# Adding the softmax row sums of four partition quadrants on VectorE instead of with a TensorE matmul, in a fused attention and convolution kernel

## Chip, cores, metric

One core of a Trainium2 chip. The metric is the device time of one execution in microseconds (us). TensorE is PE in the profile (PEld is its weight load, which runs beside the matmuls), VectorE is DVE, ScalarE is ACT, GpSimd is POOL. PSUM is the memory in which this kernel's matmuls put their results; it is handed out in buffers, here called slots. The granted clock is the share of TensorE's full speed that the profile shows as granted. Medians are of several executions.

## The reference

Sixteen images of 128 channels and 32x32 pixels pass two layers. Layer 0 is attention with four heads, each as wide as the image's 128 channels; layer 1 is two 3x3 convolutions on 4-bit inputs and weights, each followed by a batch norm over all images. Cut to what matters:

```python
def _L0_conv_ref(x, w_qkv, b_qkv, w_out, b_out):
    qkv = jnp.einsum('bchw,oc->bohw', x, w_qkv) + b_qkv[None, :, None, None]
    qkv = qkv.reshape(b, nh, 3 * c, h, w)
    q, k, v = (qkv[:, :, :c], qkv[:, :, c:2 * c], qkv[:, :, 2 * c:])
    # ... q, v to (b*nh, 1024, c), k to (b*nh, c, 1024)
    scores = jnp.einsum('bnc,bcm->bnm', q, k) * c ** (-0.5)
    attn = jax.nn.softmax(scores, axis=-1)
    out = jnp.einsum('bnm,bmc->bnc', attn, v)
    # ... heads side by side
    out = jnp.einsum('bchw,oc->bohw', out, w_out) + b_out[None, :, None, None]
    return out + x

def _L1_conv_ref(x, w1, w2, gamma1, beta1, gamma2, beta2):
    out = conv3x3(act_quant(x), weight_quant(w1))
    out = batchnorm(out, gamma1, beta1)
    out = conv3x3(act_quant(out), weight_quant(w2))
    out = batchnorm(out, gamma2, beta2)
    return out + x
```

## The kernel before

There are 64 heads (16 images of 4), and each goes through eight steps of 128 keys. In a step TensorE makes the scores `pss` (keys on partitions), ScalarE takes their exponential `e`, and TensorE gathers `psa`, the values weighted by `e`. The row sums of the softmax are not taken by TensorE: VectorE adds the eight `e` tiles into `es` (128 x 1024) and reduces `es` in transposed 32x32 blocks to `part` (128 x 32). Each 32-partition quadrant of `part` then holds a sum over its own quarter of the keys, so the four quadrants are still to be added. Before, that is the matmul `psr` with a constant `quad` of ones and zeros, which also repeats the result in every quadrant. The reciprocal, a broadcasting transpose to `rb`, and the multiply and accumulate into `acc` follow.

```python
P, Q, N, NCH, NH, B = 128, 32, 1024, 8, 4, 16
vp   = pool("vo", NCH + 3)             # 11 buffers: an image has 8 vo tiles
smp  = pool("small", 4)
ps_s = pool("ps_s", 2, space=PSUM)     # pss
ps_a = pool("ps_a", 1, space=PSUM)     # psa: one buffer for each half
ps_m = pool("ps_m", 2, space=PSUM)     # psu, psv, psr, psc share two slots
sums = once.tile([P, B * NH, N // Q], F32, name="sums")

def project_v(b, j):                   # for the next image, two tiles per head
    ps = ps_m.tile([P, NH * P], F32, tag="mm", name=f"psv_{b}_{j}")
    nc.tensor.matmul(ps, lhsT=xt[b][:, ts(j, P)], rhs=bt_sb.rearrange(...), ...)
    vos[b, j] = vp.tile([P, NH * P], F32, tag="vo", name=f"vo_{b}_{j}")
    nc.vector.tensor_copy(vos[b, j], ps)                       # L333

def attend(g, j):
    # ... psa matmuls with vos[b, j] and e; es added on VectorE
    if j == NCH - 1:
        nc.vector.tensor_copy(av[:, ts(0, HALF)], psa[g][0])   # L372
        nc.scalar.copy(av[:, ts(1, HALF)], psa[g][1])
        part = smp.tile([P, N // Q], F32, tag="part", ...)
        nc.vector.tensor_reduce(part, es..., AX.X, ALU.add, apply_transpose=True)
        es[g, "part"] = part

def normalise(g):                      # three steps after the head's last scores
    b, h = heads[g]
    ps = ps_m.tile([P, N // Q], F32, tag="mm", name=f"psr_{g}")
    nc.tensor.matmul(ps, lhsT=quad, rhs=es.pop((g, "part")), start=True, stop=True)
    rinv = sums[:, g, :]
    nc.vector.reciprocal(rinv, ps)
    rb = rbp.tile([P, N], F32, tag="rb", name=f"rb_{g}")
    nc.vector.transpose(rb, rinv.unsqueeze(2).to_broadcast([P, N // Q, Q]))
    # ... acc += av * rb; after head 3 the image is complete: x += acc + bias

# ... first convolution of finished images between the steps, the last ones at
#     the end; then a check that no sum over- or underflowed:
nc.vector.tensor_reduce(ext[:, 0:1], flat, AX.X, ALU.min)      # flat = all of sums
nc.vector.tensor_reduce(ext[:, 1:2], flat, AX.X, ALU.max)
```

The eight `vo` tiles of an image are all in use until the last head's steps come by. With 11 buffers only three tiles of the next image can be copied out early. The fourth and fifth (`psv_3`, `psv_4`) stay in the two `ps_m` slots until `attend` of the current image's fourth head frees the first `vo`. Until then no further `psv` can start.

## Time and profile before

| | before |
|---|---|
| median of 3 runs | 2197.61 us (2197.31 to 2199.77) |
| profiled span | 2195.9 us |
| mean granted TensorE clock | 0.989 |
| busy PE / DVE / ACT | 97% / 53% / 32% |

The prediction below shows lines from the timeline of TensorE of the kernel before; the columns are start, duration, engine, line, operation, tiles and shape, count, and in brackets the engine's idle time ahead of it with what ended it.

```profile
2062.54 4.13 PE L245 MATMUL psc<-pad,wq 128*128 128x512 bf16 x18
...
2079.48 5.62 PE L245 MATMUL psc<-pad,wq 128*128 128x512 bf16 x18 [8.09 <-DVE bad L473]
```

The first of these starts when TensorE has done its last `psa`: the attention is over for it. The second is the first-layer convolution of the last image, and it waits for VectorE to normalise, accumulate and quantize that image. The name `bad` is only what VectorE finished last before the start. It is the `pad` written at 2078.73 to 2079.42, just ahead of it, that the matmul reads.

### The profile page before, as it was taken

Reading aid. Unit: us, or ns where it says so; the run is one execution under the profiler, and the core shown is the slowest. Engines: PE = TensorE matmul, PEld = TensorE weight load, DVE = VectorE, ACT = ScalarE, POOL = GpSimd, SP = SyncE. Lnnn points to the kernel's source line nnn. Section 1 sums busy time; section 2 is a strip of 40 time slices with the busy share of each in tenths; the row PEclk is TensorE's granted clock in tenths of the full one; section 3 lists DMA queues with packets and bytes.
Section 4 is the critical chain, followed back from the end, with each engine's and each line's share of the span. In section 5 each row is a group of like instructions: output and inputs, shape, how many; then the busy total and the mean of one; then the engine's idle time right before and its main releaser. Section 6 shows DMA issues by size and latency. Waiting matters only on the chain.

```text
span 2195.9 us, 13805 instructions
## 1 busy us (share of the span) xinstructions
PE 2134.5 (97%) x5344; PEld 952.0 (43%) x5344; DVE 1164.1 (53%) x1218; ACT 693.2 (32%) x757; POOL 19.4 (1%) x17
## 2 busy tenths in 40 slices
PE   8999999999999999999999999999999999999883
PEld 4444444444444444444444444444444444444331
DVE  4454554645455464555545555554645555464566
ACT  2333233332323323333333323333233333333264
POOL 0000000000000000000000000000000000000002
PEclk9999999999999999999999999999999999999996
DMA  2000000000000000000000000000000000000133
GB/s 79 0 2 18 0 19 0 19 0 0 20 0 20 0 20 0 0 19 1 19 0 20 0 0 19 0 20 0 19 0 0 10 1 10 0 10 1 37 126 155
DMA packets 10297, 36.75 MB, mean 17 GB/s; under 512 B 1520, under 2 KB 1520, under 8 KB 10224
## 3 DMA queue, kind: packets, MB, share of 16 engines
q1 hardware_dynamic: 9216, 33.56, 4.1%
q10 hardware_dynamic: 1008, 2.24, 0.3%
q8 instruction: 44, 0.72, 0.1%
q14 instruction: 29, 0.24, 0.0%
HBM read 19.01 MB, written 16.78 MB: 16 GB/s over the span
## 4 chain that ended last, share of the span: by engine, by line
PE 97%; DVE 1%; ACT 1%; issue 1%; DMA 0%; DVEq 0%
PE psa L358 40%; PE pss L339 40%; PE psc L245 6%; PE psu L314 5%; PE psv L325 5%; PE psr L389 1%; ACT y L499 0%; DMA w_sb<-in_wqkv_dram 0%; DVE y L501 0%; DVE stats L256 0%; DVE ext L467 0%; DVE ext L468 0%; PE ps_at L670 0%; DVE mv L262 0%; PE ps_bt L686 0%
## 5 line engine op out<-in xcount | busy, mean ns | idle before, releaser
L358 PE MATMUL psa<-e,vo 128*128 128x512 f32 x2048 | 966.1, 594 | 0.0
L339 PE MATMUL pss<-u,x 128*128 128x512 f32 x2048 | 966.0, 593 | 0.0
L347 ACT ACTIVATE e<-pss 128x1024 f32<-128x1024 f32 x512 | 524.1, 1024 | 1308.9 <-PE pss L339 1308.9
L369 DVE TENSOR_TENSOR es<-es,e 128x1024 f32<-128x1024 f32 x384 | 467.4, 1217 | 463.5 <-ACT e L347 462.0
L339 PEld LDWEIGHTS pss<-u,x 128*128 128x128 f32 x2048 | 388.0, 190 | 482.6 <-issue 464.0
L358 PEld LDWEIGHTS psa<-e,vo 128*128 128x128 f32 x2048 | 385.4, 190 | 462.8 <-issue 460.1
L333 DVE COPY vo<-psv 128x512 f32<-128x512 f32 x128 | 88.4, 690 | 197.3 <-PE psv L325 192.9
L367 DVE TENSOR_TENSOR es<-e,e 128x1024 f32<-128x1024 f32 x64 | 78.4, 1225 | 185.2 <-ACT e L347 185.2
L245 PE MATMUL psc<-pad,wq 128*128 128x512 bf16 x576 | 134.9, 389 | 16.4 <-DVE bad L473 8.1
L314 PE MATMUL psu<-x,at_sb 128*128 128x512 f32 x256 | 132.3, 600 | 0.0
L325 PE MATMUL psv<-bt_sb,x 128*128 128x512 f32 x256 | 130.3, 593 | 0.0
L245 PEld LDWEIGHTS <-wq 128*128 128x128 bf16 x576 | 56.7, 99 | 98.6 <-issue 28.2
L395 DVE STREAM_TRANSPOSE rb<-sums 128x1024 f32<-128x1024 f32 x64 | 79.7, 1245 | 2.2
L377 DVE TRANSPOSE_TENSOR_REDUCE part<-es 128x32 f32<-128x1024 f32 x64 | 79.7, 1245 | 2.2
L314 PEld LDWEIGHTS psu<-x,at_sb 128*128 128x128 f32 x256 | 49.0, 192 | 61.4 <-issue 43.1
L325 PEld LDWEIGHTS psv<-bt_sb,x 128*128 128x128 f32 x256 | 48.3, 190 | 62.8 <-issue 52.0
L372 DVE COPY av<-psa 128x512 f32<-128x512 f32 x64 | 44.2, 691 | 46.1 <-PE psa L358 46.1
L402 DVE TENSOR_TENSOR acc<-acc,av 128x1024 f32<-128x1024 f32 x48 | 58.6, 1221 | 1.1
L252 ACT COPY y<-psc 128x512 f32<-128x512 f32 x64 | 37.5, 586 | 67.4 <-PE psc L245 66.7
L401 DVE TENSOR_TENSOR av<-av,rb 128x1024 f32<-128x1024 f32 x48 | 58.4, 1218 | 0.5
L319 DVE TENSOR_SCALAR u<-psu,au_sb 128x512 f32<-128x512 f32 x64 | 47.7, 745 | 16.3 <-PE psu L314 16.3
L256 DVE BATCH_NORM_STATS2 stats<-y 128x6 f32<-128x512 f32 x64 | 43.8, 684 | 19.9 <-ACT y L252 19.9
(69 smaller groups left out, 370.5 us busy)
## 6 DMA issues: line engine op xcount, KB each, us to landing
x<-in_x_dram SPq DMA_DIRECT2D x16, 512.0 KB, 3.5
x_dram<-x SPq DMA_DIRECT2D x16, 512.0 KB, 2.6
res<-x_dram SPq DMA_DIRECT2D x16, 512.0 KB, 10.2
out_dram<-y SPq DMA_DIRECT2D x16, 512.0 KB, 3.5
raw<-in_cw_dram ACTq DMA_DIRECT2D x2, 576.0 KB, 6.8
w_sb<-in_wqkv_dram ACTq DMA_DIRECT2D x1, 768.0 KB, 6.5
wo_sb<-in_woT_dram ACTq DMA_DIRECT2D x1, 256.0 KB, 8.8
bqkv_sb<-in_bqkv_dram ACTq DMA_DIRECT2D x1, 6.0 KB, 7.4
```

The source lines that it names most:

```text
L245: nc.tensor.matmul(ps, lhsT=wq[n][:, tap, :], rhs=pads[b % NPAD][:, r0 : r0 + RPH, dx : dx + W], start=(tap == 0), stop=(tap == NTAP - 1),)
L314: nc.tensor.matmul(ps, lhsT=at_sb[:, h, :], rhs=xt[b][:, ts(hf, HALF)], start=True, stop=True)
L325: nc.tensor.matmul(ps, lhsT=xt[b][:, ts(j, P)], rhs=bt_sb.rearrange("p h o -> p (h o)"), start=True, stop=True,)
L333: nc.vector.tensor_copy(vos[b, j], ps)
L339: nc.tensor.matmul(ps[:, ts(m, HALF)], lhsT=xt[b][:, ts(j, P)], rhs=us[g][:, ts(m, HALF)], start=True, stop=True,)
L347: nc.scalar.activation(e, ps, AF.Exp)
L358: nc.tensor.matmul(psa[g][m], lhsT=vos[b, j][:, ts(h, P)], rhs=e[:, ts(m, HALF)], start=(j == 0), stop=(j == NCH - 1),)
L367: nc.vector.tensor_tensor(es[g], es.pop((g, 0)), es.pop((g, 1)), ALU.add)
L369: nc.vector.tensor_tensor(es[g], es[g], es.pop((g, j)), ALU.add)
L377: nc.vector.tensor_reduce(part, es.pop(g).rearrange("p (k c) -> p k c", c=Q), AX.X, ALU.add, apply_transpose=True,)
L395: nc.vector.transpose(rb, rinv.unsqueeze(2).to_broadcast([P, N // Q, Q]))
L402: nc.vector.tensor_tensor(accs[b], accs[b], av, ALU.add)
```

## The change

Its intent is to take 64 matmuls, with their weight loads and their PSUM slots, out of the stream of the engine that is busy 97% of the time, and to give VectorE, which is half idle, the sum. Each quadrant is first copied to partitions 0 to 31 beside the others. A reduce adds the four, and three copies put the reciprocals back into the other quadrants.

```diff
         def normalise(g):
             b, h = heads[g]
-            ps = ps_m.tile([P, N // Q], F32, tag="mm", name=f"psr_{g}")
-            nc.tensor.matmul(ps, lhsT=quad, rhs=es.pop((g, "part")), start=True, stop=True)
+            part = es.pop((g, "part"))
+
+            side = smp.tile([Q, P // Q, N // Q], F32, tag="side", name=f"side_{g}")
+            for a in range(P // Q):
+                nc.vector.tensor_copy(side[:, a, :], part[ts(a, Q), :])
+            total = smp.tile([Q, N // Q], F32, tag="total", name=f"total_{g}")
+            nc.vector.tensor_reduce(total, side.rearrange("p a k -> p k a"), AX.X, ALU.add)
             rinv = sums[:, g, :]
-            nc.vector.reciprocal(rinv, ps)
+            nc.vector.reciprocal(rinv[0:Q, :], total)
+            for a in range(1, P // Q):
+                nc.vector.tensor_copy(rinv[ts(a, Q), :], rinv[0:Q, :])
 # ... and seven small VectorE operations that built `quad` at the start are gone
```

More of the change, by code (lines that the diff above doesn't have):

```diff
@@ L186, in general_attention, with fast_path @@
             step += 1
-def fast_path(nc, tc, x, x1d, out, at_sb, au_sb, bt_sb, bo_sb, quad, wq, sc, bnp_sb, flag, conv_weights):
+def fast_path(nc, tc, x, x1d, out, at_sb, au_sb, bt_sb, bo_sb, wq, sc, bnp_sb, flag, conv_weights):
     P = 128
@@ L631, in attention_then_quantized_convs @@
     NTAP = 9
-    Q = 32
     NCH = N // P
@@ L652, in attention_then_quantized_convs @@
     make_identity(nc, ident)
-    quad = const.tile([P, P], F32, name="quad")
-    qrow = const.tile([P, Q], F32, name="qrow")
-    nc.vector.tensor_tensor(qrow, ident[:, 0:Q], ident[:, Q : 2 * Q], ALU.add)
-    nc.vector.tensor_tensor(qrow, qrow, ident[:, 2 * Q : 3 * Q], ALU.add)
-    nc.vector.tensor_tensor(qrow, qrow, ident[:, 3 * Q : 4 * Q], ALU.add)
-    for a in range(P // Q):
-        nc.vector.tensor_copy(quad[:, ts(a, Q)], qrow)
     at_sb = const.tile([P, NH, P], F32, name="at_sb")
@@ L729, in attention_then_quantized_convs @@
     fast_path(
-        nc, tc, x, x1d, out, at_sb, au_sb, bt_sb, bo2_sb, quad, wq, sc, bnp_sb, flag, conv_weights
+        nc, tc, x, x1d, out, at_sb, au_sb, bt_sb, bo2_sb, wq, sc, bnp_sb, flag, conv_weights
     )
```

## The prediction

> **What bounds the kernel now.** I read the head of the page first, then the chain that ended last.
>
> ```profile
> PE 2134.5 (97%) x5344; PEld 952.0 (43%) x5344; DVE 1164.1 (53%) x1218; ACT 693.2 (32%) x757; POOL 19.4 (1%) x17
> ...
> PE 97%; DVE 1%; ACT 1%; issue 1%; DMA 0%; DVEq 0%
> ```
>
> TensorE (PE) is busy for 97% of the span and holds 97% of the chain. VectorE (DVE) is only 53% busy. So a change pays through what it takes from TensorE's in-order stream, and hurts only where VectorE makes TensorE wait. The source view of the removed line and the timeline of TensorE around one of its matmuls come next.
>
> ```profile
> L389 PE MATMUL psr<-part,quad x128: 190/276/297, 62.8 to 2066.5; 128*128 128x32 f32 x128
> ```
>
> ```profile
> 2040.00 1.88 PE L339 MATMUL pss<-u,x 128*128 128x512 f32 x4
> 2041.72 0.30 PE L389 MATMUL psr<-part,quad 128*128 128x32 f32 x2
> 2041.86 1.96 PE L358 MATMUL psa<-e,vo 128*128 128x512 f32 x4
> 2043.66 1.88 PE L339 MATMUL pss<-u,x 128*128 128x512 f32 x4
> ```
>
> Each of the 64 heads has two psr records. Their durations (276 ns, 35 us in all) overlap their neighbours, so I take starts. Undisturbed groups of four 128x512 matmuls follow each other at 1.717 us, 0.429 us each. Here eight of them and the psr pair fill 2040.00 to 2043.66, so the pair costs 3.66 - 8 x 0.429 = 0.23 us.
>
> At the third head of an image it looks different. TensorE, then VectorE, same stretch:
>
> ```profile
> 120.73 1.88 PE L358 MATMUL psa<-e,vo 128*128 128x512 f32 x4
> 122.45 1.88 PE L339 MATMUL pss<-u,x 128*128 128x512 f32 x4
> 124.17 1.02 PE L325 MATMUL psv<-bt_sb,x 128*128 128x512 f32 x2
> 125.02 1.88 PE L358 MATMUL psa<-e,vo 128*128 128x512 f32 x4
> 126.74 1.02 PE L339 MATMUL pss<-u,x 128*128 128x512 f32 x2
> 127.69 0.41 PE L389 MATMUL psr<-part,quad 128*128 128x32 f32 x2
> 127.93 1.10 PE L339 MATMUL pss<-u,x 128*128 128x512 f32 x2
> 128.87 1.02 PE L314 MATMUL psu<-x,at_sb 128*128 128x512 f32 x2
> ```
>
> ```profile
> 116.38 1.25 DVE L377 TRANSPOSE_TENSOR_REDUCE part<-es 128x32 f32<-128x1024 f32 x1
> 118.36 0.69 DVE L372 COPY av<-psa 128x512 f32<-128x512 f32 x1 [0.73 <-PE psa L358]
> 121.99 1.23 DVE L367 TENSOR_TENSOR es<-e,e 128x1024 f32<-128x1024 f32 x1 [2.94 <-ACT e L347]
> 123.13 0.68 DVE L333 COPY vo<-psv 128x512 f32<-128x512 f32 x1
> ```
>
> The psr pair sits inside a pss pair and costs 128.87 - 126.74 - 4 x 0.429 = 0.41 us, because it waits for a slot of the two-buffer PSUM pool (ps_m) that psv still holds. This form occurs 15 times in the timeline, the plain one 48 times, and the last pair lies in the tail. The psv at 124.17 started as soon as TensorE reached it; the vo copy that freed its slot had ended at 123.81, only 0.36 us earlier.
>
> **What the Trainium skill says.** "Perfetto Trace Analysis", section "Identifying the Most-Contended Engine", says that matmul busy time misleads because the instructions are pipelined. The trace agrees: 276 ns recorded against some 0.11 us of start-to-start per psr. "TensorE: Matmul & The Clock Gate", section "Back-to-back issue gap", says that spacing in a stream is set by weight load and matmul together. That agrees too: a psr streams only 32 columns, yet each needs a load of 128x128 weights (190 ns in the trace) that so short a matmul cannot cover. "VectorE: DVE Perf Modes", section "Two Vector instructions with no wait between them", says (as a model) that an instruction whose input or output starts in another 32-partition quadrant than the last one is held until all earlier ones have finished. No row of this trace has such copies. It does have four full-height copies in a row (quad, 128x32):
>
> ```profile
> L660 DVE COPY quad<-qrow x4: 170/172/172, 19.2 to 19.5; 128x32 f32<-128x32 f32 x4
> ```
>
> They take 172 ns each at a pitch of 0.1 us (19.2 to 19.5), so they overlap. For the new copies I choose no overlap: 0.19 us each, an estimate from the 172 ns plus some 0.02 us of gap.
>
> **The change, part by part.** It removes from TensorE 48 x 0.23 + 15 x 0.41 = 17.2 us, all on the path. It also removes the seven small copies and adds that built quad. These lie at 15.6 to 19.6 us, where psv copies have slack, so I give that nothing.
>
> It adds on VectorE, per head, four 32x32 copies, a reduce of 128 elements per partition, and three copies back; the reciprocal becomes 32x32. The reduce is an estimate from the full-row reduce L467 (2277 ns for 2048 elements, so about 144 ns fixed and 1.04 ns per element): 0.28 us. The reciprocal I leave at 0.35 us (358 ns before, at the same 32 elements a row). Together 7 x 0.172 + 0.28 = 1.48 us per head, 95 us in all: VectorE goes from 53 to about 57%. That is no bound.
>
> It moves things as well. In the build order of the changed kernel the four copies, reduce and reciprocal stand ahead of the av copy, and the back copies, transpose and both av/acc operations follow it at once; before, the latter came later. Count from the end of the part reduction (117.63), with 0.03 us for each dependent start (as from reciprocal to transpose at 2067.21 and 2067.24): four copies to 0.79, reduce to 1.10, reciprocal to 1.47, av copy to 2.1, three copies to 2.7, transpose (1.25) to 3.95, multiply (1.22) to 5.2, accumulate (1.22) to 6.45.
>
> Two places on TensorE can feel it. First, psa has one buffer, and the next head's first psa comes 3.10 us after part's end (120.73 - 117.63). The av copy ends at 2.1, so 1 us is spare: no wait, and VectorE idled 0.73 us there anyway. Second, at the third-to-fourth head boundary the order puts the vo copy that frees psv's slot behind the accumulate: it ends at 6.45 + 0.6 = 7.05 (the 0.69 us copy overlaps its predecessor by about 0.08). TensorE reaches psv at 124.17 - 117.63 = 6.54. With some 0.06 us for the signal it stalls 0.57 us, and a disturbed weight load adds about 0.1, as the 0.41 case shows. That is 0.67 x 15 = 10 us given back. One copy earlier in that queue would have avoided it.
>
> The tail: after the last head, VectorE's own chain leads through transpose, accumulate, quantize to the last first-layer conv. Before, the transpose started at 2067.24, because psr queued on TensorE behind 18 conv matmuls; part had ended at 2062.88. In the changed kernel it starts about 2.7 us after part's end, 2065.6. One more stats (0.6 us) stands ahead of the quantize there and the small flag operations move behind, so of 1.65 us about 1.3 remain.
>
> Sum: 2197.6 - 17.2 + 10 - 1.3 = 2189.1 us, 0.4% faster.
>
> **Rivals.**
> - The removal pays in full and no stall appears: 2197.6 - 18.5 = 2179 us. For it: VectorE is half idle, and if quadrant copies overlap at 0.1 us the chain shortens by 7 x 0.09 = 0.6 us, which is all of my stall. Against it: the order puts the vo copy at the end of a wholly dependent chain.
> - The small operations are slower than I think (0.3 us per copy, say, so 0.8 us more per head). Then the stall is 1.5 us x 15 = 22 us, the gain is gone, and the time is about 2201. The av copy would end at 2.6 us, still before 3.10; beyond 1 us more per head it would stall every head, at 64 us per us of excess. For it: a new kind of copy, never timed here. Against: 172 ns at four times the partitions.
> - The busy row read at face value, 35 us removed: 2162 us. The overlap of starts rules it out.
> - VectorE becomes the bound: 57% speaks against it.
>
> **Range and chances.** No stall gives 2179, a doubled one 2199. I take 2180 to 2197 for eight in ten. Faster by over 2% needs 44 us, more than the removed records hold in all: 1%. Slower by over 2% needs a wait of some 1 us in every head on top: 2%. Within 2%: 97%.
>
> **What would show it.** TensorE should have 5216 matmuls and 5216 loads, and groups following each other at 1.717 us across the places where psr stood. VectorE should have about 1723 instructions and 1258 us. 32x32 copies of about 0.17 us should start about 0.19 us apart; the av copy should start about 1.5 us after part's end, with no wait of psa for it. The decisive row is psv waiting for vo, 15 times, about 0.6 us each. If it is missing, the first rival holds; if it is over 1 us, or psa waits for av, the second. A changed granted clock (0.989) or a longer idle stretch before the last conv would make the sum wrong for reasons outside it.

## The result

| | before | after |
|---|---|---|
| median of 4 runs | 2197.76 us (2197.31 to 2199.77) | 2191.86 us (2190.98 to 2192.19) |
| ratio | | 0.9971, 95% interval 0.9953 to 0.9988 |
| profiled span | 2195.9 us | 2189.1 us |
| mean granted TensorE clock | 0.989 | 0.989 |

A ratio is the mean time of one kernel's runs over that of the other's of the same rounds, so it is not quite the ratio of the medians quoted. The changed kernel is 0.3% faster.

First the page of the kernel after (busy time by engine, then TensorE's row in the chain that ended last). They answer to the two page lines in the prediction.

```profile
PE 2122.3 (97%) x5216; PEld 938.0 (43%) x5216; DVE 1261.3 (58%) x1723; ACT 695.0 (32%) x757; POOL 19.3 (1%) x17
...
PE 89%; DVE 8%; ACT 1%; issue 1%; DMA 0%; DVEq 0%
```

PE has lost 128 records, two per head. DVE now holds 8% of the chain where it held 1%: the chain now crosses to VectorE at the boundaries. The view of TensorE's waits of the kernel after has a row that was not there before (columns: engine, line, tile, what it waited for, us in total, times, longest):

```profile
PE psv L325 <- DVE vo L333: 7.0, 15, 0.5
```

Now the same boundary as in the prediction, in the timelines of the kernel after. TensorE:

```profile
120.27 1.88 PE L358 MATMUL psa<-e,vo 128*128 128x512 f32 x4
121.98 1.88 PE L339 MATMUL pss<-u,x 128*128 128x512 f32 x4
124.33 1.12 PE L325 MATMUL psv<-bt_sb,x 128*128 128x512 f32 x2 [0.47 <-DVE vo L333]
125.30 1.88 PE L358 MATMUL psa<-e,vo 128*128 128x512 f32 x4
127.01 1.88 PE L339 MATMUL pss<-u,x 128*128 128x512 f32 x4
```

VectorE:

```profile
115.92 1.25 DVE L377 TRANSPOSE_TENSOR_REDUCE part<-es 128x32 f32<-128x1024 f32 x1
117.20 0.72 DVE L392 COPY side<-part 32x32 f32<-32x32 f32 x4
117.95 0.36 DVE L394 TENSOR_REDUCE total<-side 32x32 f32<-32x128 f32 x1
118.35 0.34 DVE L396 RECIPROCAL sums<-total 32x32 f32<-32x32 f32 x1
118.62 0.62 DVE L372 COPY av<-psa 128x512 f32<-128x512 f32 x1
119.27 0.55 DVE L398 COPY sums<-sums 32x32 f32<-32x32 f32 x3
119.85 1.25 DVE L402 STREAM_TRANSPOSE rb<-sums 128x1024 f32<-128x1024 f32 x1
121.19 1.22 DVE L408 TENSOR_TENSOR av<-av,rb 128x1024 f32<-128x1024 f32 x1
122.45 1.23 DVE L409 TENSOR_TENSOR acc<-acc,av 128x1024 f32<-128x1024 f32 x1
123.60 0.68 DVE L333 COPY vo<-psv 128x512 f32<-128x512 f32 x1
```

The `psr` pair is gone from TensorE, and `pss` at 127.01 runs undivided. But VectorE is now one unbroken chain from 115.92 to 124.28, the `vo` copy is its last link, and `psv` starts 0.05 us after that link ends. The wait is 124.33 - 121.98 - 4 x 0.429 = 0.63 us; the bracket's 0.47 is smaller because the profile's ends of matmuls are modelled and lie late. The `psv` pair then takes 125.30 - 124.33 = 0.97 us instead of 0.86, so a boundary loses 0.73 to 0.74 us.

The tail in the timeline of TensorE of the kernel after, answering to the two lines of before:

```profile
2056.58 8.10 PE L245 MATMUL psc<-pad,wq 128*128 128x512 bf16 x36
2072.23 6.11 PE L245 MATMUL psc<-pad,wq 128*128 128x512 bf16 x18 [7.55 <-DVE ok L477]
```

With these starts the whole difference of the two profiled spans can be added up:

| stretch | before | after | gained |
|---|---|---|---|
| start to the end of attention on TensorE | 2062.54 | 2056.58 | 5.96 |
| from there to the last first-layer convolution | 16.94 | 15.65 | 1.29 |
| from there to the first second-layer convolution (at 2092.92 and 2086.16) | 13.44 | 13.93 | -0.49 |
| sum, against 2195.9 - 2189.1 = 6.8 | | | 6.76 |

Of the 5.96 us, the `psr` pairs in the timeline account for 48 x 0.226 + 15 x 0.413 = 17.0 us removed, and 15 boundaries of 0.73 us for 11.0 us given back: 6.1 us expected of these two, 5.96 found. The third row is 18 convolution matmuls that took 6.11 us instead of 5.62, both at a reduced clock (0.66 and 0.72 granted over these two stretches) after the long idle time ahead of them.

### The profile page after: what moved, and what is told of

Same layout as the page of the kernel before. It is cut to its first block, busy times and chain, and to the rows that moved or that the text cites. A ratio compares the mean times of both kernels' runs of the same rounds, so it can differ in the third digit from the quotient of the medians. Undisturbed runs are those within 1.5% of the kernel's fastest.

```text
span 2189.1 us, 14211 instructions
## 1 busy us (share of the span) xinstructions
PE 2122.3 (97%) x5216; PEld 938.0 (43%) x5216; DVE 1261.3 (58%) x1723; ACT 695.0 (32%) x757; POOL 19.3 (1%) x17
## 4 chain that ended last, share of the span: by engine, by line
PE 89%; DVE 8%; ACT 1%; issue 1%; DMA 0%; DVEq 0%
PE pss L339 37%; PE psa L358 36%; PE psc L245 6%; PE psv L325 5%; PE psu L314 5%; DVE part L377 1%; DVE rb L402 1%; DVE es L369 1%; DVE av L408 1%; DVE acc L409 1%; ACT e L347 1%; DVE side L392 1%; ACT y L506 0%; DVE vo L333 0%; DVE av L372 0%
## 5 line engine op out<-in xcount | busy, mean ns | idle before, releaser
L245 PE MATMUL psc<-pad,wq 128*128 128x512 bf16 x576 | 135.5, 391 | 15.4 <-DVE pad L231 7.8
L373 ACT COPY av<-psa 128x512 f32<-128x512 f32 x64 | 37.5, 586 | 46.0 <-PE psa L358 46.0
```

The source lines that it names most:

```text
L245: nc.tensor.matmul(ps, lhsT=wq[n][:, tap, :], rhs=pads[b % NPAD][:, r0 : r0 + RPH, dx : dx + W], start=(tap == 0), stop=(tap == NTAP - 1),)
```

## The experiments

The theory: removing `psr` is worth about 17 us of TensorE's stream, and a new wait at 15 boundaries, where the `vo` copy stands last in VectorE's longer chain, gives about 11 back. Rival A: `psr` was worth only about 6 us and there is no give-back worth the name. Rival B: the small quadrant operations cost in some other place, in every head. "Before" in each result is the unchanged kernel run on the same chip in the same batch; its medians were 2198.54, 2199.11 and 2197.96 in the three batches, of nine runs each. Differences across batches carry that much of an uncertainty.

### More `vo` buffers, in both kernels

Two more `vo` buffers let `psv_3` and `psv_4` of the next image be copied out at once, so that the slots come free long before. The first kernel is the changed one with this edit, the second the kernel before with the same edit.

```diff
-        vp = pool("vo", NCH + 3)
+        vp = pool("vo", NCH + 5)
```

> The changed kernel with two more vo buffers (13 for 11), so that a psv never has to sit in PSUM for want of a vo buffer; VectorE's work is the same. Stall theory (removing psr frees 17.2 us, and 15 boundaries give back 0.63 us of wait plus 0.11 us of disturbed spacing each, 11 us): psv waits for vo vanish, about 2180.7 us, 11 us below the changed kernel. Rival A (psr was only worth some 6 us on the path, the psv wait is absorbed elsewhere): no change, about 2191. Rival B (VectorE's extra load delays TensorE diffusely): about 2190.

Measured: 2180.06 us (2179.27 to 2181.36, 5 runs), ratio 0.9916 (0.9902 to 0.9929), result correct.

> The kernel before with the same two more vo buffers, as a control for e1. Stall theory: only the 15 late psr pairs lose their slot wait, 0.41 down to 0.23 us, 15 x 0.19 = 2.8 us: about 2195. Then e2 minus e1 is the clean price of 63 psr pairs at 0.23 us plus the 0.8 us of the tail, some 15 us. Rival A: e2 minus e1 stays near 6 us. If e2 falls by 11 us as well, the buffers helped in a way of their own and e1 shows nothing about the change.

Measured: 2195.34 us (2195.01 to 2195.80), ratio 0.9984 (0.9971 to 0.9998), correct. The timeline of TensorE of the changed kernel with 13 buffers, over the same boundary:

```profile
120.91 1.88 PE L358 MATMUL psa<-e,vo 128*128 128x512 f32 x4
122.63 1.88 PE L339 MATMUL pss<-u,x 128*128 128x512 f32 x4
124.34 1.88 PE L358 MATMUL psa<-e,vo 128*128 128x512 f32 x4
126.06 1.88 PE L339 MATMUL pss<-u,x 128*128 128x512 f32 x4
```

No `psv` stands between the groups (it ran at 109.75), they follow each other at 1.717 us, and the wait for `vo` is gone from TensorE's waits. The changed kernel gained 11.8 us from the edit, the kernel before about 3 us, of which the 15 disturbed `psr` pairs (0.41 instead of 0.23) are 2.7. With the boundary out of the way the change alone is worth 2195.34 - 2180.06 = 15.3 us, close to 63 x 0.23 + 1.3 - 0.5 = 15.3. Rival A, which allows 6 us, is out.

### The one `vo` copy on another engine

Buffers change slots as well as queues. This one leaves the buffers and moves only the copy that is late.

```diff
-            nc.vector.tensor_copy(vos[b, j], ps)
+            if j == 3:
+                nc.scalar.copy(vos[b, j], ps)
+            else:
+                nc.vector.tensor_copy(vos[b, j], ps)
```

> The changed kernel, with the vo copy of the fourth chunk of each image (the one that frees psv's slot) made by ScalarE and not by VectorE; buffers as in the changed kernel. Stall theory, that the place in VectorE's queue is the cause: the psv wait goes or falls below 0.2 us, about 2181 to 2183 us. If the cause is the late release of the vo buffer itself (psa of the next head) and not VectorE's queue: the wait stays, about 2191.

Measured: 2181.01 us (2180.62 to 2182.22), ratio 0.9920 (0.9906 to 0.9933), correct; the wait is gone from TensorE's waits. Its timelines at the boundary, ScalarE and then TensorE:

```profile
122.73 0.59 ACT L334 COPY vo<-psv 128x512 f32<-128x512 f32 x1 [0.69 <-PE psa L361]
123.39 1.11 PE L325 MATMUL psv<-bt_sb,x 128*128 128x512 f32 x2
```

The copy starts when `psa` has freed the buffer, with no chain ahead of it. So it is the place of that copy in VectorE's queue that costs, not the slot as such: with the copy on ScalarE the same 11 buffers and two slots suffice. The build order moved too: `psv` now stands between two `pss` pairs, earlier in TensorE's stream than in the changed kernel, and still doesn't wait. It costs 0.09 us more than undisturbed there, 15 x 0.09 = 1.3 us, about what this version is slower than the one with 13 buffers. This repair needs no memory.

### `psr` taken out and nothing put in its place

The reciprocal is taken of each partition's own part. It is made from the kernel before, so the small operations that build `quad` stay. The result is wrong (relative error 0.044).

```diff
-            # side copies, reduce, reciprocal of total, copies back
+            nc.vector.reciprocal(rinv, es.pop((g, "part")))
```

> Wrong result on purpose: psr is taken away and the reciprocal is taken of each partition's own partial sums, so nothing is added on VectorE. Stall theory: the full 17.2 us of TensorE are gained; the vo copy comes 1.5 us earlier, before TensorE reaches psv, so no stall; and the tail's transpose starts 0.4 us after part's end, not 2.6 us as in the changed kernel or 4.4 us as before, some 3 us: about 2177 us. Rival A: about 2190.

Measured: 2181.74 us (2179.50 to 2182.39), ratio 0.9921 (0.9908 to 0.9935). This missed by 4 to 5 us. The order of the build had put an addition to `es` ahead of the `vo` copy, so `psv` still started 0.09 us late and ran 0.1 us longer: about 15 x 0.19 = 2.8 us. Another 0.9 us is the batch, whose kernel before took 2198.54 us and not 2197.6. The tail did what was expected: from the end of attention to the last first-layer convolution it took 2061.67 - 2047.74 = 13.93 us, 3.0 less than the 16.94 of before. The remaining 1 us is within the spread of these runs. It is therefore no clean upper limit. It says only that leaving the quadrant work out, and changing the order by that, does no better than keeping the work and moving one copy (2181.01).

### More copies, as a dose

Three, then eight copies more per head ahead of the four (the surplus ones write tiles that are written again).

```diff
-            for a in range(P // Q):
+            for a in [i % 4 for i in range(3)] + [0, 1, 2, 3]:
```

> The changed kernel with three of the quadrant copies done twice (seven for four), 0.18 us each, so some 0.5 us more in VectorE's chain per head. The order puts an es add in place of the accumulate ahead of the vo copy, which gives 0.1 back. Stall theory: only the 15 boundaries pay, each 0.45 us more: psv waits about 0.9 us for vo, 2191.9 + 7 = about 2199 us, slower than the kernel before. If the extra load delayed every head, 64 x 0.54 = 35 us: about 2226. If the wait is not caused by this chain: no change.

Measured: 2196.45 us (2196.22 to 2196.81), ratio 0.9989 (0.9975 to 1.0002), correct: 4.6 us slower than the changed kernel, and no longer shown to differ from the one before. The wait at a boundary rose from 0.63 to 1.04 us, 15 x 0.41 = 6.2 us; the profiled span rose by 2194.1 - 2189.1 = 5.0. The order of the tail moved too (its long idle time fell from 7.55 to 5.92 us), which returned 1.6, and the convolution after it took 0.7 longer.

> The same with eight extra copies (twelve for four): 1.44 us more per head. Stall theory: the 15 psv waits grow by about 1.3 us to some 1.8 us: 2191.9 + 20 = about 2212 us; the av copy stands behind the copies but still ends before psa's next use, 2.8 us against 3.1 us after part's end, so psa never waits. If every head pays: 2191.9 + 92 = 2284.

The edit is the same with `range(8)`. Measured: 2228.78 us (2228.09 to 2228.89), ratio 1.0136 (1.0120 to 1.0151), correct. Expected had been 2212, so this missed by 17 us. The wait itself grew as forecast (by 1.45 us, with 1.3 expected); the miss lies in what follows. Timeline of TensorE of this kernel at the boundary:

```profile
122.13 1.88 PE L339 MATMUL pss<-u,x 128*128 128x512 f32 x4
125.93 1.12 PE L325 MATMUL psv<-bt_sb,x 128*128 128x512 f32 x2 [1.93 <-DVE vo L333]
126.89 3.39 PE L358 MATMUL psa<-e,vo 128*128 128x512 f32 x4
130.07 2.11 PE L339 MATMUL pss<-u,x 128*128 128x512 f32 x4
132.03 1.02 PE L314 MATMUL psu<-x,at_sb 128*128 128x512 f32 x2
```

TensorE stood idle for 125.93 - 122.13 - 1.717 = 2.08 us. Then a group of four `psa` took 130.07 - 126.89 = 3.18 us instead of 1.717. The view of busy times by stretch, for 126 to 131 us, gives the granted clock in the column after POOL:

```profile
126.00:131.00 5.00, 5.00 (x8) 2.15 (x9) 2.83 (x3) 0.00 (x0) 0.00 (x0) 0.66 0.00 0
```

The clock was 0.66 in this stretch, where the changed kernel has 1.00. The same stretch reads 0.66 again from 648, 1170 and 1693 us, so it happened at 4 of the 15 boundaries, every fourth, and cost 3.18 + 1.96 - 2 x 1.717 = 1.7 us each. The excess over the changed kernel, in profiled spans 2226.2 - 2189.1 = 37.1 us, adds up like this:

- longer waits, 15 x (2.08 - 0.63) = 21.8 us;
- low clock, 4 x 1.7 = 6.8 us;
- in 50 heads `psa` started about 0.05 us late, presumably for the `av` copy that had just ended, and ran on some 0.07 longer, 5.9 us;
- the tail's idle time, 9.18 instead of 7.55, 1.6 us.

That makes 36.1; 1.0 us stays unexplained. The two doses also show how steep the boundary is: 5 us for three copies, 37 for eight. The kernel with three copies has waits of 1.04 us and no drop of the clock at the boundaries. No run tries a wait between 1.04 and 2.08.

### Eight more copies, with more `vo` buffers

> The eight extra copies of e6, with the 13 vo buffers of e1. e6 came 37 us above the changed kernel where 20 were expected. Stall theory, amended: in e6 the 15 psv waits are 2.08 us each (22 us more than in the changed kernel), the clock drops after a few of them (some 5 us), and the rest (some 7 us) are psa waits of about 0.12 us in each of 48 heads and a longer tail. With 13 buffers only that rest stays: 2180.1 + 7 = about 2187 us, clock 0.989. If e6's excess is the copies' load as such: about 2217.

The edit is the two above together. Measured: 2187.91 us (2186.89 to 2189.14, 4 runs), ratio 0.9952 (0.9937 to 0.9967), correct. With the boundary free, eight further copies in every head cost only 2187.91 - 2180.06 = 7.9 us, and the same `psa` start 0.05 us late is still in the timeline. The granted clock stays at 1.00 through the attention: without the idle time at the boundary there is no drop. VectorE works 2.38 - 0.72 = 1.66 us more per head (twelve copies against four, in the timeline), 106 us in all, and 98 of them are hidden. Rival B is out for the change itself, whose work is smaller: in its timeline no group of `psa` starts late except behind the 15 `psv`.

### `psr` put back, its result unread

The changed kernel with 13 `vo` buffers, and the `psr` matmul back in its place in the stream, with the small operations that build `quad`. VectorE still does the sum.

```diff
             part = es.pop((g, "part"))
+            ps = ps_m.tile([P, N // Q], F32, tag="mm", name=f"psr_{g}")
+            nc.tensor.matmul(ps, lhsT=quad, rhs=part, start=True, stop=True)
```

> The kernel of e1 (changed, with 13 vo buffers, 2180.1 us) with the psr matmul put back on TensorE and its result read by nobody; VectorE keeps its quadrant copies. It prices psr on TensorE by itself. Stall theory: 63 x 0.23 = 14 us on top, about 2194 us. Rival A (psr worth some 6 us on the path): about 2186. Busy time taken at face value (276 ns x 128): 35 us, 2215.

Measured: 2195.63 us (2194.43 to 2195.89), ratio 0.9983 (0.9970 to 0.9997), correct. Against 2180.06 without it that is 15.6 us, 15.0 after the shift between the batches, or about 0.24 us for each of 63 pairs. The source view of the matmul in this run, min, median and max in ns:

```profile
L390 PE MATMUL psr<-part,quad x128: 190/233/276, 63.7 to 2064.6; 128*128 128x32 f32 x128
```

Two records per head of 233 ns, but not 30 us: the records overlap their neighbours. Starts, not durations, give the price.

### All four side copies from the same quadrant

Every copy reads quadrant 0 of `part` and writes partitions 0 to 31. The sum is four times one quadrant's sum and so wrong.

```diff
-                nc.vector.tensor_copy(side[:, a, :], part[ts(a, Q), :])
+                nc.vector.tensor_copy(side[:, a, :], part[0:Q, :])
```

> Wrong result on purpose: the four side copies of the changed kernel all read the first quadrant and write the same first quadrant, everything else alike. If, as the Trainium skill's model says, a copy is held only when its start quadrant differs from the last one's, these four overlap at a pitch of 0.1 us and not 0.18: the chain is 0.24 us shorter, the 15 psv waits drop from 0.63 to about 0.4 us, about 2188 us. If small copies of 32 partitions never overlap: pitch 0.18 us and 2191.9 us.

Measured: 2186.40 us (2185.80 to 2186.93), ratio 0.9942 (0.9928 to 0.9956). In the timeline of VectorE of this kernel the four copies read:

```profile
116.81 0.42 DVE L392 COPY side<-part 32x32 f32<-32x32 f32 x4
```

0.42 us instead of 0.72, with the same size and number: copies from one quadrant start about 0.08 us apart ((0.42 - 0.17) / 3 = 0.08), copies from changing quadrants 0.18 us ((0.72 - 0.17) / 3). The wait at the boundary fell by exactly that, from 0.63 to 0.33 us.

### A contiguous reduce

The side copies write with a step of four elements, so that the reduce can read in one run.

```diff
-            side = smp.tile([Q, P // Q, N // Q], F32, tag="side", name=f"side_{g}")
+            side = smp.tile([Q, N // Q, P // Q], F32, tag="side", name=f"side_{g}")
-                nc.vector.tensor_copy(side[:, a, :], part[ts(a, Q), :])
+                nc.vector.tensor_copy(side[:, :, a], part[ts(a, Q), :])
-            nc.vector.tensor_reduce(total, side.rearrange("p a k -> p k a"), AX.X, ALU.add)
+            nc.vector.tensor_reduce(total, side, AX.X, ALU.add)
```

> The changed kernel with side laid out so that the reduce reads its four values next to each other; the copies write with a stride of four. The reduce took 0.365 us where 0.28 were predicted. If the strided read is the cause: 0.28 us, psv waits 0.63 down to 0.55 us, 2191.9 - 1.3 = about 2190.6 us. If the 32 short outputs are the cause: 0.365 us and no change.

Measured: 2191.07 us (2190.41 to 2191.39, 4 runs), ratio 0.9966 (0.9951 to 0.9981), correct. The reduce in the source view, in the kernel after and in this one:

```profile
L394 DVE TENSOR_REDUCE total<-side x64: 357/365/365, 57.0 to 2058.1; 32x32 f32<-32x128 f32 x64
```

```profile
L394 DVE TENSOR_REDUCE total<-side x64: 274/274/274, 57.3 to 2058.1; 32x32 f32<-32x128 f32 x64
```

The same 128 elements take 365 ns when neighbours are 128 bytes apart and 274 ns in one run. But the four copies rose from 0.72 to 0.78 us (185 ns each instead of 170), and the wait only fell from 0.63 to 0.60 us. The layout is of no use by itself; no difference in time is shown.

### The best version, and its counterpart without the change

The changed kernel with 13 `vo` buffers, the contiguous reduce, and one edit in the tail: the minimum and maximum over the sums are taken early for the first 60 heads, and at the end for the last four alone, so that two reduces of 2.28 us leave the chain to the last convolution.

```diff
+        def extremes(i, g0, g1):
+            flat = sums[:, g0:g1, :].rearrange("p g k -> p (g k)")
+            nc.vector.tensor_reduce(ext[:, i : i + 1], flat, AX.X, ALU.min)
+            nc.vector.tensor_reduce(ext[:, 2 + i : 3 + i], flat, AX.X, ALU.max)
+
+        at(n_steps - 20, extremes, 0, 0, len(heads) - 4)
 # ... at the end, in place of the two reduces over all heads:
+        extremes(1, len(heads) - 4, len(heads))
```

> A version meant to beat both: e1 with the contiguous reduce, and with the overflow check's two reductions over all sums (2.28 us each, one of them on the last chain before the quantize) done in advance for the first 60 heads and at the end for the last four only. The stretch from the last part to the last first-layer conv should fall from 15.3 to about 11.6 us, and TensorE idles about 4 and not 7.5 us there: 2180.1 - 3.7 = about 2176 us, a little less if the clock drops less.

Measured: 2177.34 us (2175.94 to 2178.48, 4 runs), ratio 0.9902 (0.9887 to 0.9917), correct. It has the lowest median of all kernels run here, 20.6 us under the kernel before of its batch, though its interval overlaps that of the buffer edit alone. Timeline of TensorE in its tail:

```profile
2058.13 6.87 PE L245 MATMUL psc<-pad,wq 128*128 128x512 bf16 x18 [3.92 <-DVE bad L487]
```

The idle time fell from 7.55 to 3.92 us, but the 18 matmuls after it took 6.87 us instead of 6.11, at a granted clock of 0.59 instead of 0.66, so part of it was lost again to the clock.

> The control for e11: the kernel before (psr on TensorE) with the 13 vo buffers and the same tail. If the change's worth is what the ledger says, 63 psr pairs of 0.23 us and some 1 us of tail, it is 15 us above e11: about 2191 us. If the tail edit takes away what the change gained at the end: 13 to 14 us.

The counterpart is the kernel before with 13 buffers and the same tail. Measured: 2192.73 us (2190.91 to 2193.05), ratio 0.9971 (0.9957 to 0.9985), correct. The change is worth 2192.73 - 2177.34 = 15.4 us between these two, as it was (15.3) between the two kernels with only the buffers edited. The tail edit is worth 2.6 to 2.7 us in both kernels (2195.34 to 2192.73 and 2180.06 to 2177.34, across batches).

## Why the prediction was right

It said 2189.1 us in a range of 2180 to 2197; measured were 2191.86, and its mechanism is what the runs show.

- The price of `psr` (0.23 us plain, 0.41 us disturbed, 17.2 in all): 17.0 by the timeline. Putting the matmul back without the boundary cost 15.0 to 15.6 us, for 63 plain pairs. That the disturbed pairs waited for a slot is shown by the kernel before with 13 buffers, where all 63 are plain. The 35 us of the busy row were rightly refused. The page of the Trainium skill that the prediction cites on busy time ("Perfetto Trace Analysis", section "Identifying the Most-Contended Engine") gives as its reason that pipelined TensorE instructions look smaller in the trace; here they looked larger (276 ns recorded, 0.11 us from start to start).
- The stall of `psv` (0.57 + 0.1 us, 15 times, 10 us): measured 0.63 + 0.10, 11.0 us. The accumulate ended 6.51 us after `part` (6.45 predicted), the `vo` copy 7.11 (7.05). That "one copy earlier in that queue would have avoided it" was not run as such; moving that copy to ScalarE did avoid it.
- The terms in that chain: side copies at a pitch of 0.18 us (0.19 predicted), reciprocal 341 ns (350). The one mis-sized is the reduce, 365 ns instead of 280. Its estimate came from a reduce that reads its row in one run; the contiguous variant measured 274. (Its split into 144 ns and 1.04 ns per element cannot come from the one row that it names; the one-element `ok<-ext` in the same trace, 0.14 us, supports it.) That the error hardly shows is luck: shorter copies made up for it, and the `av` copy ended 2.07 us after `part` with 2.1 predicted.
- The `av` copy started 118.62 - 117.17 = 1.45 us after `part` ended (1.5 predicted), and no `psa` waited for it. VectorE: 1723 instructions and 1261 us (1258).
- The tail: 1.29 us gained (1.3). Not foreseen: the slower clock in the convolution after it, 0.49 us.

The final number was 2.8 us low. About 1 us is the larger stall and 0.5 the tail's clock. The rest, some 1.3 us, is not resolved by the runs, whose spread is of the same size: the two profiled spans differ by 6.8 us, the medians by 5.9.

The first rival (removal in full, no stall, 2179) failed for the reason given against it, and two repairs brought the time to 2180.06 and 2181.01. The second, that slow small copies turn the gain into loss, was right in kind: three surplus copies per head took back more than half of the gain by the medians (ratio 0.9989 against 0.9971), and eight turned it into a loss (1.0136).

## What to carry to other kernels

When work is taken off the busiest engine, look in the new order for what that engine waits on and now stands behind the moved work: here one PSUM copy, last in a chain of 7 us, took back 11 of 17 us, and either two more buffers or another engine for that copy returned them. Price small matmuls in a full stream by the starts of their neighbours, not by their recorded durations (0.23 us per pair here, against 0.55). Work that is hidden nearly everywhere (106 us of extra copies, 98 of them free) can still be dear at one boundary per image.

## What the Trainium skill lacked or had wrong

- "TensorE: Matmul & The Clock Gate", section "Why this matters for your kernels", advises against idle gaps over about 3 us. In the run with eight more copies an idle time of 2.08 us was followed by a clock of 0.66 (mean of 5 us) at 4 of 15 boundaries, each costing 1.7 us; with the same copies and no idle time there was no drop. A shorter gap can already cost, in some of its occurrences.
- "VectorE: DVE Perf Modes", section "Two Vector instructions with no wait between them", says when an instruction is held but gives no price for it. The runs agree with the rule and show the price: 32x32 copies of 170 ns start 0.18 us apart when the quadrant changes from one to the next, and about 0.08 us apart when it doesn't (0.72 against 0.42 us for four).
- "SBUF — State Buffer", section "Door 1: The DMA port swizzle", says in a note that each access that crosses to a new 16-byte line pays a penalty, without a figure. VectorE took 365 ns to reduce 128 fp32 elements that lie 128 bytes apart and 274 ns for the same in one run; a 32-element copy that writes 16 bytes apart took 185 ns instead of 170.
